# Turning rows with the DMA's transpose instead of TensorE in a feed-forward phase

## The chip, the cores and the metric

The kernel runs on one core of a Trainium2 chip. The core has five engines with queues of their own, which run side by side and wait for each other through semaphores: TensorE (PE in the profile), VectorE (DVE), ScalarE (ACT), GpSimd (POOL) and SyncE (SP), which here only starts DMAs. The metric is the time of one execution in microseconds of device time, as the median of several runs.

## The reference

64 sequences of 64 tokens, each token a row of 256 numbers (4096 rows in all), pass four layers. Each sequence b has a condition vector of 64 numbers.

1. A gated feed-forward layer with a quantized down projection, added to its input.
2. Attention with 16 heads inside each sequence, added to its input; and then the feed-forward that this document is about: with r = x / rms(x), gamma and beta vectors of the sequence,
   `x = x + alpha_b * ((silu(n Wg) * (n Wh)) Wo + bo)`, where `n = gamma_b * r + beta_b`. Wg and Wh are 256 x 1024, Wo is 1024 x 256.
3. A layer norm over the 256 numbers of a row, times a weight, plus a bias and a tanh vector of the sequence, times the weight again, plus the bias.
4. An adapter whose weights depend on the sequence: `x + relu(x Wd_b + bd) Wu_b + bu`, with Wd_b of 256 x 128 and Wu_b of 128 x 256.

Everything is float32. The large products are made of three matmuls each: both factors are split into a high part, rounded to the type fp32r, and the rest, and high x high, high x low and low x high are summed.

## The kernel before

The rows are worked in 8 blocks of 512. The first layer fills the first 255 us, attention the time to about 430 us, and the feed-forward with layer norm and adapter the rest. The change lies in that last phase.

There the main loop runs over n = 8 i + f: block i (0 to 7), and f (0 to 7), an eighth of the 1024 inner columns. The first five n are written out ahead of the loop. In iteration n:

- `f_inner` calls `f_products`: 12 matmuls of 512 columns on PE make the gate and the hidden half (`pg`, `pv`). ACT takes the silu of `pg` into `sg` (L816), DVE multiplies it by `pv` (L819).
- `f_parts` splits `sg`: ACT casts the high part (`hhi`, L856), DVE subtracts it (`hlo`, L857).
- `f_outer(n - 2)`: 12 matmuls of 256 columns add the columns of two iterations ago into `acc`.

Between these, spread over the iterations f, stands the work of other blocks:

- For block i+1, the rows are loaded (`f_load`, f=0), squared and summed by ACT with a root by POOL (`f_begin`, f=1), scaled by ACT into `xn` (`f_scale`, f=3), and turned in `norm_turn` for the two halves c of the 256 columns (f=5 and f=6): four PE transposes of 128 x 128 into a PSUM bank (L262), DVE's multiply by gamma into `xg` (L265), POOL's addition of beta (L266). At the head of the next iteration the function in `late` runs: ACT casts `xh` (L245) and POOL subtracts for `xl` (L246). The next block's products need both.
- For block i-1, DVE scales `acc` by alpha into `x3` (f=1), adds the input and takes the row statistics (f=1, f=2); POOL makes the root; DVE makes the shift `nm` (L896) and ACT centres four tiles (L898) in `f_center` (f=2); `f_adapt` (f=4, f=5) turns `x3` by four PE transposes per half (L933) between products and silu, and DVE scales the result into `x4` (L934).
- In f=7 PE runs one half of the up products of block i-2 (L979), then the down products of block i-1 from `x4` (`f_down`, L963), then the other up half. ACT takes the relu `dn`; DVE finishes `yo` (L995) and SP stores it.
- POOL adds common parts to the loaded adapter weights (`f_common`, L924: `wd` at f=7 and f=0, `wu` at f=3 and f=4) and to the block's input (`f_base`, f=7).

The order on PE, DVE, ACT and POOL is the order of the source (`manual_schedule`), also in the attention and feed-forward phases. SP is not among these engines after the opening part: there a scheduler puts its DMAs into an order of its own. Each queue runs in order, so an instruction that waits holds all behind it. Block 0 has no block before it, and in block 7 (`more` is false) nothing is prepared; its end is `f_last`.

The first layer already uses the DMA's transpose, for the 128 x 1024 quantized rows in bf16 (`quant`, L483), issued by SP. That transpose works on 16-bit elements.

Of the kernel before, what the change touches and what calls it, by code (L numbers as in the profile page):

```python
# [8 lines left out]
F32 = mybir.dt.float32  # L9
F32R = mybir.dt.float32r  # L10
BF16 = mybir.dt.bfloat16
AF = mybir.ActivationFunctionType
ALU = mybir.AluOpType
AX = mybir.AxisListType
# [3 lines left out]
P = 128  # L18
NB = 64
L = 64  # L20
D = 256
NTOK = NB * L
T = 512
NBLK = NTOK // T
BB = T // L
TT = T // P
# [10 lines left out]
def tile_kernel(ctx: ExitStack, tc, xT, x, condT, cw, upT, downT, qkvT, woT, ghT, outT_w,  # L37
                vecs, rows, g1, g2, gb, out):
    nc = tc.nc
# [12 lines left out]
    pools = {}  # L52
# [38 lines left out]
    def b3(ap):  # L91
        return ap.rearrange("p (b l) -> p b l", l=L)
# [165 lines left out]
    def norm_turn(xn, hl, i, c, vg, vb):  # L258

        pt = bank("mm")  # L260
        for t in range(TT):
            nc.tensor.transpose(pt[:, t * P:(t + 1) * P], xn[:, t, c * P:(c + 1) * P], ident)  # L262
        uid[0] += 1
        xg = main.tile([P, T], F32, tag="xg", bufs=2, name=f"xg{uid[0]}")
        nc.vector.tensor_tensor(b3(xg), b3(pt), bc(vg, c, i), ALU.mult)  # L265
        nc.gpsimd.tensor_tensor(b3(xg), b3(xg), bc(vb, c, i), ALU.add)  # L266
        return lambda: split(hl, c, xg, nc.gpsimd)

# [507 lines left out]
    def f_load(i):  # L776
        x2 = block(f"fx2_{i}")
        nc.sync.dma_start(out=x2, in_=tok(x2d, i))
        fblk[i] = dict(x2=x2)

    def f_begin(i):
        fblk[i]["rs"] = rms(fblk[i]["x2"], f"f{i}")

    def f_scale(i):
        fblk[i]["n"] = norm_tm(fblk[i]["x2"], fblk[i]["rs"], f"f{i}", True)
# [26 lines left out]
    def f_inner(n, between=lambda: None):  # L812
        pg, pv = f_products(n)
        between()
        sg = main.tile([P, T], F32, tag="st", bufs=2, name=f"sg{n}")
        nc.scalar.activation(sg, pg, AF.Silu)  # L816
        if n == LAST:
            return sg, pv
        nc.vector.tensor_tensor(sg, pv, sg, ALU.mult)  # L819
        return sg  # L820
# [71 lines left out]
    def f_center(i, tiles, rs):  # L892
# [3 lines left out]
        nc.vector.scalar_tensor_tensor(nm[:, :n], B["mv"][:, t0:t0 + n, 0], -1.0, rs[:, :n], ALU.mult, ALU.mult)  # L896
        for k, t in enumerate(tiles):
            nc.scalar.activation(B["x3"][:, t], B["x3"][:, t], AF.Identity, bias=nm[:, k:k + 1], scale=rs[:, k:k + 1])  # L898

# [27 lines left out]
    def f_adapt(i, c):  # L927
        B = fblk[i]
        if c == 0:
            B["x4"] = pools["c"].tile([P, 2, T], F32, tag="x4", bufs=2, name=f"x4_{i}")  # L930
        pt = bank("mm")
        for t in range(TT):
            nc.tensor.transpose(pt[:, t * P:(t + 1) * P], B["x3"][:, t, c * P:(c + 1) * P], ident)  # L933
        nc.vector.scalar_tensor_tensor(b3(B["x4"][:, c]), b3(pt), w2[:, c:c + 1], bc(V_LIN, c, i),  # L934
                                       ALU.mult, ALU.add)

    def f_turn(i, k):

# [241 lines left out]
    gbt = pools["c"].tile([P, 4, D], F32, tag="yo", bufs=1, name="gbt")  # L1180
    nc.sync.dma_start(out=gbt, in_=gb)
    late = []
    for n in range(5, N):
        i, f = divmod(n, 8)
        more = i + 1 < NBLK
# [4 lines left out]
        if i > 0 and f == 2:  # L1190
            f_added(i - 1, 1)
            f_stats(i - 1, 1)
            rln = rsqrt(fblk[i - 1]["mv"][:, :, 1], 1.0, 1e-5, f"ln{i - 1}")
        if i > 0 and f in (4, 5):
            sg = f_inner(n, lambda: f_adapt(i - 1, f - 4))
        else:
            sg = f_inner(n)
        if more and f in (5, 6):
            late = [norm_turn(*fblk[i + 1]["n"], i + 1, f - 5, V_FG, V_FB)]
        up = i - 2 if more and f == 7 else i - 2 if not more and f == 0 else -1  # L1200
        if up >= 0:
# [15 lines left out]
        if i > 0:  # L1217
            if f == 1:
                for k in range(2):
                    f_scaled(i - 1, k)  # L1220
                f_added(i - 1, 0)
                f_stats(i - 1, 0)
            if f == 2:
                f_center(i - 1, range(TT), rln)
        if i > 0 and more:
            if f == 0:
                f_load(i + 1)
            if f == 1:
                f_begin(i + 1)
            if f == 3:  # L1230
                f_scale(i + 1)
        if f == 2 and i > 0:
            f_rows(i)

        if f == (6 if more else 1):
            f_weights(i, "wd")
        if f == (7 if more else 1):
            f_weights(i, "wu")
# [70 lines left out]
```

## Time and profile before

| what | us |
|---|---|
| median of 3 runs | 743.86 (742.52 to 744.04) |
| the profiled execution | 743.25 |
| its span, first to last instruction | 741.5 |
| PE busy | 731.8 |
| DVE, ACT, POOL busy | 534.7, 412.6, 339.6 |
| DVE, ACT, POOL busy from 566 to 605, about one block | 22.54, 16.56, 20.87 |

A line of the timeline begins with the start and the duration in us, then the engine, the line of the source, the operation, what is written and read, the shapes, the number of merged instructions, and in brackets how long the engine stood idle before it and what released it. In a line of a group, the number before the comma behind the bar is the time in sum and the one behind it the mean in ns. Matmuls are pipelined: their durations overlap, and the distance of their starts says how fast they go.

### The profile page before, as it was taken

The numbers are of one execution on the slowest core, as the hardware profiler recorded it, in microseconds if no ns is written. First come the engines' busy times: TensorE is split into PE (matmuls) and PEld (weight loads), VectorE is DVE, ScalarE is ACT, GpSimd is POOL, SyncE is SP. The second block draws the span as 40 slices with busy tenths as digits, with TensorE's granted clock in tenths as the row PEclk, the third lists the DMA queues.
The fourth block names the chain that finished last, engine by engine and source line by source line (L and its number), as shares of the span: only waits on it lengthen the run. The fifth ranks groups of instructions, "written<-read, shape, count | busy, mean of one in ns | idle before, by whom it ended". The sixth has DMA issues, their size and how long they took to land.

```text
span 741.5 us, 17485 instructions
## 1 busy us (share of the span) xinstructions
PE 731.8 (99%) x7036; PEld 613.3 (83%) x7036; DVE 534.7 (72%) x827; ACT 412.6 (56%) x865; POOL 339.6 (46%) x359
## 2 busy tenths in 40 slices
PE   9999999999999999999999999999999999999997
PEld 8876766776686878998988888888889888888886
DVE  4998878867587688888888866656565555656566
ACT  6553446446455588998899674535353434434242
POOL 2123133143235436655555437464646464545292
PEclk9999999999999999999999999999999999999999
DMA  8898899999995974455665237713171809080821
GB/s 265 245 263 170 275 258 253 305 276 250 216 281 119 193 187 114 127 138 140 158 152 130 74 105 187 157 47 97 46 184 31 197 6 223 1 199 3 224 61 59
DMA packets 117457, 118.88 MB, mean 160 GB/s; under 512 B 39632, under 2 KB 101200, under 8 KB 117376
## 3 DMA queue, kind: packets, MB, share of 16 engines
q1 hardware_dynamic: 109232, 91.29, 50.4%
q0 software_dynamic: 7488, 25.37, 11.4%
q8 instruction: 55, 0.90, 0.5%
q10 hardware_dynamic: 656, 1.11, 0.5%
q14 instruction: 26, 0.21, 0.1%
HBM read 71.41 MB, written 29.56 MB: 136 GB/s over the span
## 4 chain that ended last, share of the span: by engine, by line
PE 83%; DVE 9%; ACT 3%; issue 2%; DMA 1%; POOL 0%; ACTq 0%; DVEq 0%; POOLq 0%
PE gh L89 7%; PE gh L88 7%; PE gh L87 7%; PE mm L87 6%; PE mm L89 6%; PE mm L88 6%; PE acc L87 4%; PE acc L88 4%; PE acc L89 4%; PE m L87 3%; PE m L89 3%; PE m L88 3%; PE mm L495 3%; PE m L712 3%; PE mm L304 3%; PE S L671 2%
## 5 line engine op out<-in xcount | busy, mean ns | idle before, releaser
L87 PE MATMUL mm<-up,xhl 128*128 128x512 f32 x240 | 97.2, 405 | 0.0
L87 PE MATMUL gh<-xhf,gh 128*128 128x512 f32 x244 | 95.3, 390 | 0.0
L89 PE MATMUL gh<-xhf,gh 128*128 128x512 f32 x244 | 95.1, 390 | 0.0
L88 PE MATMUL gh<-xlf,gh 128*128 128x512 f32 x244 | 95.1, 390 | 0.0
L89 PE MATMUL mm<-up,xll 128*128 128x512 f32 x240 | 93.9, 391 | 0.0
L88 PE MATMUL mm<-up,xhl 128*128 128x512 f32 x240 | 93.6, 390 | 0.0
L819 DVE TENSOR_TENSOR sg<-gh,sg 128x512 f32<-128x512 f32 x60 | 41.3, 688 | 62.1 <-PE gh L89 34.8
L469 ACT ACTIVATE g<-mm,rs_l 128x512 f32<-128x512 f32 x64 | 43.9, 690 | 69.8 <-PE mm L89 47.0
L857 DVE TENSOR_TENSOR hlo<-sg,hhi 128x512 fp32r<-128x512 f32 x58 | 56.2, 969 | 35.0 <-ACT hhi L856 33.7
L856 ACT CAST hhi<-sg 128x512 fp32r<-128x512 f32 x58 | 35.9, 620 | 76.4 <-DVE sg L819 75.2
L87 PE MATMUL acc<-wout,hhi 128*128 128x256 f32 x248 | 72.1, 291 | 0.0
L470 DVE SCALAR_TENSOR_TENSOR h<-mm,rs_l,g 128x512 f32<-128x512 f32 x64 | 46.4, 745 | 33.4 <-PE mm L89 24.0
L89 PE MATMUL acc<-wout,hlo 128*128 128x256 f32 x248 | 69.4, 280 | 0.6 <-DVE hlo L854 0.6
L88 PE MATMUL acc<-wout,hhi 128*128 128x256 f32 x248 | 69.4, 280 | 0.0
L266 POOL TENSOR_TENSOR xg<-xg,cv 128x512 f32<-128x512 f32 x32 | 33.1, 1042 | 65.8 <-DVE xg L265 65.8
L87 PEld LDWEIGHTS mm<-up,xhl 128*128 128x128 f32 x240 | 45.1, 188 | 15.2 <-issue 2.4
L89 PEld LDWEIGHTS gh<-xhf,gh 128*128 128x128 f32 x244 | 45.8, 188 | 9.7
L89 PEld LDWEIGHTS mm<-up,xll 128*128 128x128 f32 x240 | 45.0, 188 | 10.1
L88 PEld LDWEIGHTS mm<-up,xhl 128*128 128x128 f32 x240 | 45.2, 188 | 8.5
L88 PEld LDWEIGHTS gh<-xlf,gh 128*128 128x128 f32 x244 | 45.8, 188 | 7.3
L87 PEld LDWEIGHTS gh<-xhf,gh 128*128 128x128 f32 x244 | 45.8, 188 | 7.3
L816 ACT ACTIVATE sg<-gh 128x512 f32<-128x512 f32 x61 | 35.9, 589 | 26.1 <-PE gh L89 26.1
(259 smaller groups left out, 1930.3 us busy)
## 6 DMA issues: line engine op xcount, KB each, us to landing
gt<-in_g SPq DMA_DIRECT2D x32, 512.0 KB, 7.5
rows<-alphad SPq DMA_DIRECT2D x48, 256.0 KB, 5.5
vb<-vx SPq DMA_DIRECT2D x32, 256.0 KB, 5.3
wd<-s1d SPq DMA_DIRECT2D x32, 256.0 KB, 6.1
wu<-s2d SPq DMA_DIRECT2D x32, 256.0 KB, 6.0
xt<-in_x SPq DMA_DIRECT2D x8, 512.0 KB, 7.6
s1d<-stgs POOLq DMA_DIRECT2D x16, 256.0 KB, 7.0
s1d<-stg POOLq DMA_DIRECT2D x16, 256.0 KB, 6.9
```

The costliest lines, as they stand in the source:

```text
L87: nc.tensor.matmul(out, lhsT=l[0], rhs=r[0], start=first, stop=False)
L88: nc.tensor.matmul(out, lhsT=l[0], rhs=r[1], start=False, stop=False)
L89: nc.tensor.matmul(out, lhsT=l[1], rhs=r[0], start=False, stop=last)
L266: nc.gpsimd.tensor_tensor(b3(xg), b3(xg), bc(vb, c, i), ALU.add)
L304: nc.tensor.matmul(pb[s][c * 64:(c + 1) * 64], lhsT=gl[h], rhs=gt[h, c * GC:(c + 1) * GC], start=True, stop=True, tile_position=(64 * s, 6 ...
L469: nc.scalar.activation(g, pg, AF.Gelu, scale=rs[:, t:t + 1])
L470: nc.vector.scalar_tensor_tensor(h[:, ch * 512:(ch + 1) * 512], pv, rs[:, t:t + 1], g, ALU.mult, ALU.mult)
L495: nc.tensor.matmul(py[:, :D], lhsT=qt[:, f, :], rhs=wq[:, f, :], start=f == 0, stop=f == 7)
L816: nc.scalar.activation(sg, pg, AF.Silu)
L819: nc.vector.tensor_tensor(sg, pv, sg, ALU.mult)
L856: nc.scalar.copy(h_hi, sg)
L857: nc.vector.tensor_tensor(h_lo, sg, h_hi.bitcast(F32), ALU.subtract)
```

## The change

In the feed-forward loop the PE transposes of the next block's rows (blocks 2 to 7) and of the adapter's input (blocks 0 to 6) are replaced by three steps.

- `split_words`: ACT copies a float32 tile of 128 x 1024 as 16-bit words, all low halves and then all high halves, into `planes`: two instructions of 1024 elements.
- `turn_words`: SP issues two DMA transposes from SBUF to SBUF, one for each set of halves, into `turned`.
- `join_words`: for each half c of the columns, DVE copies 1024 16-bit words so that low and high halves stand side by side again, as 512 float32 numbers.

`norm_joined` takes the place of `norm_turn`: join, DVE's multiply in place, POOL's addition, and the same function for `late`. `f_adapt` joins into `x4` and then scales in place. Where the steps stand in a block i between 1 and 6:

| step | before | after |
|---|---|---|
| load of rows | block i+1 at f=0 | block i+2 at f=4 |
| squares and root | block i+1 at f=1 | block i+2 at f=7 |
| scale into `xn` | f=3 | f=0 |
| split and transposes of rows | - | f=1 |
| turned rows to `xg`, both halves | f=5, f=6, between sg and the split of n | f=4, f=5, behind the split of n |
| shift `nm` | f=2 | f=2 |
| centring on ACT | f=2, at the end | f=3, between silu and the cast of n |
| split and transposes of `x3` | - | f=4 |
| `x4`, both halves | f=4, f=5, PE between products and silu | f=6, at the end |
| `wd` loads | f=6 | f=5 |

In block 0 the rows of block 1 are still turned by PE, and block 2 is loaded at f=5. In block 7 the steps of `x3` stand at the same f. `planes` and `turned` take buffers that attention used. From n = 5 on SP too follows the order of the source.

```diff
+    def split_words(src, name):
+        planes = pools["b"].tile([P, 16, L], F32, tag="ex2", bufs=2, name=f"planes_{name}")
+        dst = planes.rearrange("p a l -> p (a l)").bitcast(U16).rearrange("p (h c t f) -> p h c t f", h=2, c=2, t=TT)
+        words = src.rearrange("p t d -> p (t d)").bitcast(U16).rearrange("p (t c f h) -> p h c t f", t=TT, c=2, h=2)
+        for h in range(2):
+            nc.scalar.copy(dst[:, h], words[:, h])
+        return planes
+    def turn_words(planes, name):
+        turned = pools["b"].tile([P, 2, 512], F32, tag="pts", bufs=2, name=f"turned_{name}")
...
+        for h in range(2):
+            nc.sync.dma_start_transpose(out=dst[:, h], in_=src[:, h])
+        return turned
+    def join_words(dst, turned, c):
+        src = turned.rearrange("p c n -> p (c n)").bitcast(U16).rearrange("p (h c n) -> p h c n", h=2, c=2)
+        nc.vector.tensor_copy(dst.bitcast(U16).rearrange("p (n h) -> p h n", h=2), src[:, :, c])
+    def norm_joined(hl, turned, i, c, vg, vb):
+        xg = main.tile([P, T], F32, tag="xg", bufs=2, name=f"xg{uid[0]}")
+        join_words(xg, turned, c)
+        nc.vector.tensor_tensor(b3(xg), b3(xg), bc(vg, c, i), ALU.mult)
         nc.gpsimd.tensor_tensor(b3(xg), b3(xg), bc(vb, c, i), ALU.add)
         return lambda: split(hl, c, xg, nc.gpsimd)
...
-        pt = bank("mm")
-        for t in range(TT):
-            nc.tensor.transpose(pt[:, t * P:(t + 1) * P], B["x3"][:, t, c * P:(c + 1) * P], ident)
-        nc.vector.scalar_tensor_tensor(b3(B["x4"][:, c]), b3(pt), w2[:, c:c + 1], bc(V_LIN, c, i),
-                                       ALU.mult, ALU.add)
+        x4 = B["x4"][:, c]
+        join_words(x4, B["turned"], c)
+        nc.vector.scalar_tensor_tensor(b3(x4), b3(x4), w2[:, c:c + 1], bc(V_LIN, c, i), ALU.mult, ALU.add)
...
+    ordered.close()
+    ordered.enter_context(tc.manual_schedule(engines=engines | {E.SP}))
     for n in range(5, N):
...
-        if i > 0 and f in (4, 5):
-            sg = f_inner(n, lambda: f_adapt(i - 1, f - 4))
-        else:
-            sg = f_inner(n)
-        if more and f in (5, 6):
-            late = [norm_turn(*fblk[i + 1]["n"], i + 1, f - 5, V_FG, V_FB)]
+        sg = f_inner(n)
+        if i == 0 and f in (5, 6):
+            late = [norm_turn(*fblk[1]["n"], 1, f - 5, V_FG, V_FB)]
+        if i > 0 and f == 3:
+            f_center(i - 1, range(TT), rln, shift)
...
             if f == 2:
-                f_center(i - 1, range(TT), rln)
+                shift = f_shift(i - 1, range(TT), rln)
+            if f == 4:
+                fblk[i - 1]["turned"] = turn_words(split_words(fblk[i - 1]["x3"], f"x{i - 1}"), f"x{i - 1}")
+            if f == 6:
+                for c in range(2):
+                    f_adapt(i - 1, c)
         if i > 0 and more:
             if f == 0:
-                f_load(i + 1)
+                f_scale(i + 1)
             if f == 1:
-                f_begin(i + 1)
-            if f == 3:
-                f_scale(i + 1)
+                fblk[i + 1]["turned"] = turn_words(split_words(fblk[i + 1]["n"][0], f"n{i + 1}"), f"n{i + 1}")
+            if f in (4, 5):
+                late = [norm_joined(fblk[i + 1]["n"][1], fblk[i + 1]["turned"], i + 1, f - 4, V_FG, V_FB)]
+        if i + 2 < NBLK:
+            if f == (4 if i else 5):
+                f_load(i + 2)
+            if f == 7:
+                f_begin(i + 2)
...
-        if f == (6 if more else 1):
+        if f == (5 if more else 1):
             f_weights(i, "wd")
```

More of the change, by code (lines that the diff above doesn't have):

```diff
@@ L11 @@
 BF16 = mybir.dt.bfloat16
+U16 = mybir.dt.uint16
 AF = mybir.ActivationFunctionType
@@ L265, in norm_turn @@
         nc.vector.tensor_tensor(b3(xg), b3(pt), bc(vg, c, i), ALU.mult)
+        nc.gpsimd.tensor_tensor(b3(xg), b3(xg), bc(vb, c, i), ALU.add)
+        return lambda: split(hl, c, xg, nc.gpsimd)
+    def split_words(src, name):
[7 more added lines that the diff above has]
+        turned = pools["b"].tile([P, 2, 512], F32, tag="pts", bufs=2, name=f"turned_{name}")
+        src = planes.rearrange("p a l -> p (a l)").bitcast(U16).rearrange("p (h n) -> p h n", h=2)
+        dst = turned.rearrange("p c n -> p (c n)").bitcast(U16).rearrange("p (h k r) -> p h k r", h=2, k=8)
+        for h in range(2):
[5 more added lines that the diff above has]
+    def norm_joined(hl, turned, i, c, vg, vb):
+        uid[0] += 1
+        xg = main.tile([P, T], F32, tag="xg", bufs=2, name=f"xg{uid[0]}")
+        join_words(xg, turned, c)
+        nc.vector.tensor_tensor(b3(xg), b3(xg), bc(vg, c, i), ALU.mult)
         nc.gpsimd.tensor_tensor(b3(xg), b3(xg), bc(vb, c, i), ALU.add)
@@ L810, in f_products, with f_inner @@
         return pg, pv
-    def f_inner(n, between=lambda: None):
+    def f_inner(n):
         pg, pv = f_products(n)
-        between()
         sg = main.tile([P, T], F32, tag="st", bufs=2, name=f"sg{n}")
@@ L890, in f_stats, with f_shift @@
             nc.vector.bn_aggr(B["mv"][:, t], B["st"][:, t])
-    def f_center(i, tiles, rs):
+    def f_shift(i, tiles, rs):
         B, n, t0 = fblk[i], len(tiles), tiles[0]
@@ L896, in f_center @@
         nc.vector.scalar_tensor_tensor(nm[:, :n], B["mv"][:, t0:t0 + n, 0], -1.0, rs[:, :n], ALU.mult, ALU.mult)
+        return nm
+    def f_center(i, tiles, rs, nm=None):
+        B = fblk[i]
+        nm = f_shift(i, tiles, rs) if nm is None else nm
         for k, t in enumerate(tiles):
```

## The prediction

> **What bounds the kernel now.** I read the page first: its busy times and the chain that ended last.
>
> ```profile
> span 741.5 us, 17485 instructions
> PE 731.8 (99%) x7036; PEld 613.3 (83%) x7036; DVE 534.7 (72%) x827; ACT 412.6 (56%) x865; POOL 339.6 (46%) x359
> ...
> PE 83%; DVE 9%; ACT 3%; issue 2%; DMA 1%; POOL 0%; ACTq 0%; DVEq 0%; POOLq 0%
> ```
>
> PE is busy throughout and carries 83% of the chain. The same chain in order of time gives the rhythm of the feed-forward phase: the adapter's down products (L963) come once a block.
>
> ```profile
> 604.65 1.08 PE mm L979 x32
> 605.74 1.87 PE mm L963 x64
> 607.60 0.93 PE mm L979 x32
> 643.53 1.08 PE mm L979 x32
> ```
>
> A block lasts 643.53 - 604.65 = 38.9 us, and in this phase the chain stays on PE to the last block. Then the timeline, PE first, to price a transpose:
>
> ```profile
> 521.97 0.39 PE L89 MATMUL gh<-xhf,gh 128*128 128x512 f32 x1
> ...
> 522.20 0.60 PE L262 MATMUL mm<-ident,xnf 128*128 128x128 f32 x4
> ...
> 522.55 0.37 PE L87 MATMUL acc<-wout,hhi 128*128 128x256 f32 x1
> ...
> 522.75 0.28 PE L88 MATMUL acc<-wout,hhi 128*128 128x256 f32 x1
> ```
>
> Durations of matmuls overlap, so the start times count: four transposes put the next product 0.35 us later, and 0.08 us more are lost at the change of kind. By the starts of the gate products, an iteration without a turn takes 4.13 us, with one 4.56, with two 5.03.
>
> Last the other engines, where a turned row passes DVE, POOL and ACT:
>
> ```profile
> 596.97 0.68 DVE L819 TENSOR_TENSOR sg<-gh,sg 128x512 f32<-128x512 f32 x1
> 597.57 0.68 DVE L265 TENSOR_TENSOR xg<-mm,cv 128x512 f32<-128x512 f32 x1
> 598.34 1.58 DVE L857 TENSOR_TENSOR hlo<-sg,hhi 128x512 fp32r<-128x512 f32 x1
> ...
> 598.32 1.04 POOL L266 TENSOR_TENSOR xg<-xg,cv 128x512 f32<-128x512 f32 x1 [6.37 <-DVE xg L265]
> ...
> 599.39 0.62 ACT L245 CAST xhf<-xg 128x512 fp32r<-128x512 f32 x1 [1.09 <-POOL xg L266]
> 599.92 0.59 ACT L816 ACTIVATE sg<-gh 128x512 f32<-128x512 f32 x1
> ```
>
> Two things are to be seen. ACT's silu (L816) waits in its queue behind the cast of the turned rows (L245), and so for POOL's add and DVE's multiply. And a DVE instruction with two SBUF inputs (L857) that starts beside a POOL one takes 1.58 us, where it takes 0.69 alone: it ran after POOL's.
>
> **What is removed.** 48 transposes of block rows (L262 has 56 in this phase, the 8 for block 1 stay) and 56 of the adapter (L933): 26 groups of four. Blocks 1 to 6 have four groups each, by the iterations above 2 x (4.56 - 4.13) + (5.03 - 4.13) = 1.75 us; block 7 has two, 0.9. Sum 6 x 1.75 + 0.9 = **-11.4 us**, all on the path, since PE has no other idle time there.
>
> **What is added.** The groups of 1024 elements, shapes kept apart:
>
> ```profile
> L684 DVE TENSOR_TENSOR ex<-S,mx 128x1024 f32<-128x1024 f32 x32 | 39.2, 1224 | 1.1
> L481 DVE TENSOR_SCALAR q<-h 128x1024 bf16<-128x1024 f32 x32 | 24.1, 754 | 1.1
> ...
> L689 ACT ACTIVATE ex<-ex 128x1024 f32<-128x1024 f32 x32 | 34.1, 1066 | 12.4 <-DVE ex L684 12.4
> ```
>
> ACT: 26 splits of 1024 elements, by L689 1.07 us each; 4.3 us a block beside 16.6 busy of 39. DVE: 26 joins of 1024 16-bit elements, from SBUF to SBUF with one input. Rows from both sides: L481, one input, in SBUF, 0.69 as its median; L684, from PSUM, 1.22. The join has one input and both ends in SBUF, as L481, so I take 0.69 and keep 1.22. The multiplies that follow had PSUM and SBUF inputs and now have two in SBUF; their durations stay (0.68, 0.74), but they can meet POOL. SP: 26 transposes of the shape of the existing one:
>
> ```profile
> L483 SPq DMA_TRANSPOSE qt<-q x32: 1231/1358/5807, 23.0 to 250.2; - x32
> ...
> DMA to landing us min/median/max: 3.0/5.9/17.8
> ```
>
> That is 1.36 us of SP each and 5.9 to landing, in a phase where the DMA engines are 94% busy; in the feed-forward phase they are 45% busy.
>
> **What moves.** On SP the source order now holds. In block i: two transposes of rows (f=1), four row loads (f=2), two of the adapter (f=4), then the block load, four wd loads, and at f=7 two stores and four wu loads. The load of block i+2 and the wd loads stand behind the adapter's transposes, which wait for ACT. By the walk below these are issued by 25.5 us, five issues of about 0.6 follow, and wd lands (6.1) near 35; POOL wants it past 40, behind the root that follows the squares of f=7. Cost nothing; without that cover POOL's bias adds slip, and they have a block's length to spare. The 30 us that SP spent on row loads waiting for POOL (L277) go, and nobody on the path waited for them. The squares (f=1 to f=7), the scale (f=3 to f=0) and the centring (behind the silu of f=3) keep their ACT time; PE doesn't wait for them directly.
>
> **Where it hurts: the order on DVE and ACT.** Before, PE turned the rows while DVE was between sg and hlo, and the adapter input was ready at f=5. Now the join stands behind hlo in f=4 and f=5, and both adapter joins behind hlo(6), right before PE's down products of f=7 want them. I walk one block from its first gate product (571.09 in the trace), without transposes: iteration f starts at 4.13 f, f=7 at 28.9, and down is due after products and one up half: 28.9 + 2.83 + 0.98 = 32.7.
> The centring's shift ends at 17.1 and centring at 19.2, as now (L896, L898). ACT then casts hhi(3), 19.8, and DVE subtracts, 20.5, so sg(4) starts at 20.4. From sg to the next free DVE slot behind hlo is 1.98 (594.32 to 596.30). Join 0.62 with its handover, multiply to POOL 0.75 (597.57 to 598.32), POOL to cast 1.07, cast to silu 0.53, silu to sg 0.63: one loop is 5.6 us against 4.13 of PE. So sg(5) at 26.0 and sg(6) at 31.6; hlo(5) falls on POOL's wu adds or its subtraction and pays the 0.89 seen above: 32.45. Then hlo(6) ends and the joins begin at 34.45; join, x4, join, x4 (0.62, 0.66, 0.62, 0.75) end at 37.1. PE waits 37.1 - 32.7 = **4.4 us in each of blocks 2 to 6**, and 5.4 in block 1, which has no up half before it: 27.4 us. Behind the waiting down products stand the other up half and the outer products of f=5; behind the joins on DVE sg(7) and both yo, so a late transpose would hold these too. Bounds of one wait: 3.5 if hlo(5) meets no POOL instruction; 6.5 with joins of 1.22; 9 if two more instructions wait for a POOL add of 1.26 each.
>
> **The tail.** In block 7 the adapter's four DVE instructions stand before the last sg. DVE now waits 0.62 us there, so 2.7 - 0.6 = 2.1 us come on top; POOL adds without pause then, and each of the four may wait up to 1.26: up to 7. I take **+4**.
>
> **PE's clock.** It is 1.00 in all rows. The longest PE gap now is 1.65 us (before 228.07), and the products after it start 0.23 us apart, the full rate. At the start of the span, after idling, matmuls of the transposes' shape (L507) start 0.24 apart, where transposes take 0.09, and the full rate comes at about 9 us. So a gap of 4.4 costs between 0 and half of those 8 us, 4; I take 1 each, near the 1.65 us gap, **+6**.
> [...]
>
> **Sum.** -11.4 + 27.4 + 4 + 6 = +26.0 on the profiled execution of 743.25 (span 741.5 and 1.75 around it): 769.3. The median of the runs is 0.6 above that execution: **770 us**, 3.5% slower.
>
> **Rivals.** (a) No wait: DVE's 22.5 busy us of a block grow only to 25.3 of 37.1, and if the queues ran ahead of PE the gain would stand: 743.9 - 11.4 + 2.1 = 735. Against it: the loop of 5.6 us is a chain, not a load. It decides below (11.4 - 4) / 6 = 1.2 us of wait per block. Chance 0.08. (b) Joins at one element a cycle, 1.22: waits 6 x 6.5 + 1 = 40, so 743.9 - 11.4 + 40 + 5 + 6 = 783. For: strided 16-bit output, which no row has. 0.2. (c) The clock falls fully at each wait, 4 instead of 1: 770 + 18 = 788. 0.12. (d) The adapter's transposes land late: the second is issued at about 24.5 and joined at 34.45, so from 10 us on it decides; at the worst row, 17.8, each block waits 8 more: 770 + 48 = 818. Against: idle DMA engines. 0.07. (e) Gain and wait cancel: 744. 0.02. The forecast holds the other 0.51.
>
> **Range.** 0.2%, 1.5 us, is about what runs from 742.52 to 744.04 can tell from no change. Low end: waits of 3.5 (22), tail 2.1, no clock loss: 743.9 + 12.7 = 757, a little below it for shorter lag; high end: (b) and most of (c) together, 798. 754 to 798 leaves out (a), (d) and (e). Slower is (b), (c), (d) and the forecast: 0.9; faster is (a).
>
> **What would show it.** After: no L262 or L933 transposes past block 1; PE gaps before L963 in blocks 1 to 6, released by DVE's x4, of 4 to 6 us, and a block of 37.1 + 4.4 = 41.5 us; joins at 0.69; silu late behind the cast in f=5 and f=6; a granted clock below 1.00 if (c). It would be wrong if x4 came before PE's up half ended, or if the wait's releaser were a DMA.

## The result and the profile after

The changed kernel takes 787.4 us (median of 4 runs, 786.8 to 788.5) where the kernel before takes 743.5 (742.5 to 744.0): a ratio of 1.059, with a 95% interval of 1.0575 to 1.0612. It is 5.9% slower. Ratios here and below leave out runs over 1.5% above their kernel's fastest, of which there is one. The prediction had the sign and the place, and was 17 us short.

The profiled execution has a span of 785.0 us, 43.5 more than the 741.5 before. The page of the kernel after, first the busy times, then the granted clock in 40 slices, then the chain that ended last:

```profile
span 785.0 us, 17412 instructions
...
PE 737.5 (94%) x6932; PEld 618.7 (79%) x6932; DVE 555.2 (71%) x853; ACT 435.0 (55%) x891; POOL 346.8 (44%) x359
...
PEclk9999999999999999999999999898989899897998
...
PE 59%; DVE 19%; issue 9%; ACT 6%; POOL 5%; DMA 2%; DVEq 0%; ACTq 0%; POOLq 0%
```

PE's share of the chain falls from 83% to 59%; DVE's rises from 9% to 19%, ACT's from 3% to 6% and POOL's from 0% to 5%. PE's busy time is no smaller although 104 transposes are gone: the clock row, which was full speed throughout, has a dent about once per block from the 26th slice on (0.50 from 535.34 to 542.16 us in block 2), and matmuls take longer in it.

One block of the timeline of the kernel after, PE around f=7 (start, duration, what, and in brackets the idle time and its releaser). L1015 are the up products, L999 the down products:

```profile
531.44 1.15 PE L1015 MATMUL mm<-dn,wu 128*64 128x64 f32 x32
536.35 0.48 PE L999 MATMUL mm<-x,wd 128*64 128x64 f32 x4 [3.76 <-issue]
537.75 3.47 PE L999 MATMUL mm<-x,wd 128*64 128x64 f32 x60 [0.91 <-DVE x L971]
541.00 1.63 PE L1015 MATMUL mm<-dn,wu 128*64 128x64 f32 x32
```

PE waits for the first half of x4, does four matmuls, waits for the second half, and then runs slowly. (The profile names no releaser for the first gap, "issue"; DVE's multiply that completes this half, L971, ends at 536.25.) The two gaps are 3.76 + 0.91 us; with the four matmuls between them the down products are held up for about 5 us. After them the second up half takes 1.56 us by the starts, where it took 1.03 before. The table of windows shows why (columns: the stretch, its length, busy time and instructions of PE, PEld, DVE, ACT and POOL, granted clock, DMA share, GB/s):

```profile
527.00:532.60 5.60, 5.59 (x58) 4.67 (x56) 3.10 (x3) 1.28 (x3) 2.85 (x4) 1.00 0.98 274
532.60:536.30 3.70, 0.00 (x0) 0.00 (x0) 2.84 (x5) 1.22 (x3) 0.96 (x1) 0.87 0.00 0
536.30:541.00 4.70, 3.74 (x65) 3.58 (x66) 2.62 (x4) 0.00 (x0) 0.00 (x0) 0.50 0.15 56
541.00:544.00 3.00, 3.00 (x48) 2.93 (x47) 0.84 (x2) 1.32 (x3) 0.00 (x0) 0.81 0.02 5
```

The clock drops to one half near the end of the wait and stays there through the down products: by the three windows' shortfalls, (0.13 x 3.7 + 0.5 x 4.7 + 0.19 x 3.0) / 0.5 = 6.8 us at half speed.

What PE waits for is best read in the chain of waits in order of time (start, length, what), here for the block that ends near 677 us:

```profile
656.88 1.05 POOL xg L299
...
657.95 0.02 ACT xhf L246
657.97 0.50 issue
658.48 0.60 ACT sg L848
...
659.10 0.70 DVE sg L851
...
659.83 0.63 ACT hhi L888
...
660.48 1.73 DVE hlo L889
662.21 0.67 DVE xg L291
...
662.90 0.70 DVE xg L298
...
663.68 1.05 POOL xg L299
...
667.88 0.74 DVE x L291
```

This is the loop of the prediction, in one piece: POOL's addition, ACT's cast (L246) and the silu behind it (L848), sg, hhi, hlo on DVE, the join (L291), the multiply (L298), and POOL again. This turn takes 663.68 - 656.88 = 6.8 us, where PE's iteration takes 4.13; it is the dearer of two, because hlo meets POOL's subtraction and takes 1.73, where it takes 0.69 alone. The turn before it, from sg(4) to sg(5), takes 5.8. The two together put the adapter's joins behind the time at which the down products are due.

The new instructions themselves, from the groups with their shapes kept apart (mean ns of one behind the busy time):

```profile
L291 DVE COPY x<-turned_x 128x1024 uint16<-128x1024 uint16 x14 | 14.6, 1042 | 0.0
...
L291 DVE COPY xg<-turned_n 128x1024 uint16<-128x1024 uint16 x12 | 9.0, 749 | 0.0
...
L276 ACT COPY planes_x<-x 128x1024 uint16<-128x1024 uint16 x13 | 13.0, 1042 | 0.0
```

The same join is on average dearer for the adapter than for the rows: four of the fourteen, in block 6 and the tail, take 1.8 us, the others 0.73 to 0.74. The tail shows the reason, DVE beside POOL's bias additions, and PE behind it:

```profile
757.83 1.85 DVE L291 COPY x<-turned_x 128x1024 uint16<-128x1024 uint16 x1
759.71 1.60 DVE L971 SCALAR_TENSOR_TENSOR x<-x,w,cv 128x512 f32<-128x512 f32 x1
761.24 1.80 DVE L291 COPY x<-turned_x 128x1024 uint16<-128x1024 uint16 x1
763.07 1.59 DVE L971 SCALAR_TENSOR_TENSOR x<-x,w,cv 128x512 f32<-128x512 f32 x1
...
765.49 0.58 PE L88 MATMUL acc<-wout,hhi 128*128 128x256 f32 x1 [5.31 <-ACT hhi L884]
```

Where the time went, by the starts of products. Each f=7 stretch is from the gate products of f=7 to those of the next f=0.

| stretch | before | after | difference |
|---|---|---|---|
| iterations with turns (26 groups of four transposes) | | | -11.4 |
| f=7 of block 1 | 6.34 | 14.55 | +8.2 |
| f=7 of blocks 2 to 5, each | 8.20 | 15.4 | 4 x 7.2 = +28.8 |
| f=7 of block 6 | 8.20 | 19.32 | +11.1 |
| tail: block 7's last outer products, to the start of the down products | 5.87 | 13.02 | +7.15 |
| sum | | | +43.9 |

The spans differ by 43.5.

### The profile page after: what moved, and what is told of

The parts are those of the page before. It is cut to its first block, busy times and chain, and to the rows that moved or that the text cites. A ratio compares the mean times of both kernels' runs of the same rounds, so it can differ in the third digit from the quotient of the medians.

```text
span 785.0 us, 17412 instructions
## 1 busy us (share of the span) xinstructions
PE 737.5 (94%) x6932; PEld 618.7 (79%) x6932; DVE 555.2 (71%) x853; ACT 435.0 (55%) x891; POOL 346.8 (44%) x359
## 4 chain that ended last, share of the span: by engine, by line
PE 59%; DVE 19%; issue 9%; ACT 6%; POOL 5%; DMA 2%; DVEq 0%; ACTq 0%; POOLq 0%
PE mm L88 6%; PE mm L90 6%; PE mm L89 6%; PE m L88 3%; PE m L90 3%; PE m L89 3%; PE m L745 3%; PE mm L528 3%; PE gh L90 3%; PE gh L89 3%; PE gh L88 3%; PE mm L337 3%; PE mm L999 3%; POOL wu L962 2%; PE acc L88 2%
## 5 line engine op out<-in xcount | busy, mean ns | idle before, releaser
L889 DVE TENSOR_TENSOR hlo<-sg,hhi 128x512 fp32r<-128x512 f32 x58 | 51.9, 895 | 53.2 <-ACT hhi L888 53.0
L999 PE MATMUL mm<-x,wd 128*64 128x64 f32 x448 | 25.5, 302 | 34.2 <-issue 20.6
L88 PEld LDWEIGHTS acc<-wout,hhi 128*128 128x128 f32 x248 | 47.3, 191 | 7.9 <-ACT hhi L884 5.5
L90 PEld LDWEIGHTS gh<-xhf,gh 128*128 128x128 f32 x244 | 45.8, 188 | 9.6
L962 POOL TENSOR_TENSOR wd<-wd,bias 128x512 f32<-128x512 f32 x32 | 52.1, 1649 | 0.0
L999 PEld LDWEIGHTS mm<-x,wd 128*64 128x64 f32 x448 | 23.4, 210 | 36.4 <-issue 21.4
```

Of the source, the lines that this page charges most:

```text
L88: nc.tensor.matmul(out, lhsT=l[0], rhs=r[0], start=first, stop=False)
L90: nc.tensor.matmul(out, lhsT=l[1], rhs=r[0], start=False, stop=last)
L889: nc.vector.tensor_tensor(h_lo, sg, h_hi.bitcast(F32), ALU.subtract)
L962: nc.gpsimd.tensor_tensor(w[:, 2 * h:2 * h + 2], w[:, 2 * h:2 * h + 2], row.unsqueeze(1).broadcast_to([P, 2, D]), ALU.add)
L999: nc.tensor.matmul(pd[s * 64:(s + 1) * 64, (b - b0) * L:(b - b0 + 1) * L], lhsT=B["wd"][b // 4][:, b % 4, c, s * 64:(s + 1) * 64], rhs=B[" ...
```

## The experiments

All ratios are to the kernel before, with 95% intervals. "After" is the changed kernel.

### The clock: work put into the wait

```diff
 def f_down(i, half=None):
     pd = bank("mm" if half is None else "acc")
+    for _ in range(22 if i + 2 < NBLK else 0):
+        nc.tensor.matmul(pd, lhsT=pools["gh"][0][:, 0, :P], rhs=fblk[i + 1]["n"][1][0][:, 0], start=True, stop=True)
```

> The changed kernel with 22 matmuls of 128x512 added ahead of the down products of blocks 0 to 5, into the bank that the down products then overwrite: they give PE about 5 us of work (22 at 0.23 us) in the time in which it would wait for x4, and leave the result alone. Theory (idle time halves the clock, and the half clock costs 2 to 2.5 us behind each wait): the granted clock stays at 1.00 in blocks 1 to 6, the 64 down products take 1.9 us again instead of 4.65 and the total falls by 8 to 14 us although work is added: 773 to 779. Rival (the products behind the wait are slow for another reason, such as cold weights loads or x4's arrival): 786 to 792, down products at 4.6 us as now.

Measured: 778.2 us (777.4 to 782.7), ratio 1.048 (1.045 to 1.051). With 132 matmuls added the kernel is 9 us faster than after. PE of this kernel, the fillers in the first line, and a window over a block and a half:

```profile
533.20 5.28 PE L997 MATMUL mm<-xhf,gh 128*128 128x512 f32 x22
538.41 0.34 PE L1001 MATMUL mm<-x,wd 128*64 128x64 f32 x4
539.29 1.97 PE L1001 MATMUL mm<-x,wd 128*64 128x64 f32 x60 [0.54 <-DVE x L971]
541.09 1.10 PE L1017 MATMUL mm<-dn,wu 128*64 128x64 f32 x32
```

```profile
540.00:600.00 60.00, 60.00 (x509) 52.96 (x506) 33.74 (x58) 29.40 (x60) 31.73 (x26) 1.00 0.53 124
```

The clock is 1.00 and 60 down products take 1.8 us by the starts (539.29 to 541.09) instead of 3.25 (537.75 to 541.00). In blocks 3 to 5 the f=7 stretch falls from 15.4 to 13.5. So of the 7.2 us that a block loses there, 1.9 are the clock's and 5.3 are the wait itself. The expectation was not met everywhere: in blocks 1 and 6, where gaps of 1.8 and 4.1 us in sum were left, the clock still fell for 3.4 us.

### One half of the change at a time

Rows only (the adapter on PE as before):

```diff
-        sg = f_inner(n)
+        sg = f_inner(n, lambda: f_adapt(i - 1, f - 4, True)) if i > 0 and f in (4, 5) else f_inner(n)
...
-            if f == 4:
-                fblk[i - 1]["turned"] = turn_words(split_words(fblk[i - 1]["x3"], f"x{i - 1}"), f"x{i - 1}")
-            if f == 6:
-                for c in range(2):
-                    f_adapt(i - 1, c)
```

> The block rows keep their DMA transposes, splits and joins; the adapter's input is turned by PE again in f=4 and f=5, between products and sg, as before the change (its splits and DMA transposes are left out). Theory: the adapter's joins at the end of f=6 are what PE waits for; without them the down products find x4 ready, the PE wait of 4.9 us and the lower clock of blocks 1 to 6 go, the tail is as before (5.9 us), and of the 11.4 us that the removed transposes were worth the rows' half, 5.3, is kept: 736 to 742. Rival (the join of the rows behind hlo slows the loop of sg by itself, so that PE waits for hhi or hlo in the outer products instead): 750 to 775, with the wait moved to the outer products of f=6 and f=7.

Adapter only (the rows on PE as before):

```diff
-        if i == 0 and f in (5, 6):
-            late = [norm_turn(*fblk[1]["n"], 1, f - 5, V_FG, V_FB)]
+        if more and f in (5, 6):
+            late = [norm_turn(*fblk[i + 1]["n"], i + 1, f - 5, V_FG, V_FB)]
...
-            if f == 1:
-                fblk[i + 1]["turned"] = turn_words(split_words(fblk[i + 1]["n"][0], f"n{i + 1}"), f"n{i + 1}")
-            if f in (4, 5):
-                late = [norm_joined(fblk[i + 1]["n"][1], fblk[i + 1]["turned"], i + 1, f - 4, V_FG, V_FB)]
```

> The adapter's input keeps its DMA transposes, splits and joins at the end of f=6; the block rows are turned by PE again in f=5 and f=6, with the multiply between sg and hlo, as before the change (their splits and DMA transposes are left out). Theory (both together make the wait: rows delay sg(6), adapter joins stand behind it): sg(6) is on time, joins begin near 33 us of the block and end near 36, and the down products are due near 33.5, so a wait of 1.5 to 3 us is left in a block, too short to lower the clock; the tail keeps its 7 us: 748 to 768. Rival 1 (the adapter's joins alone make the whole wait): waits of 5 us, clock lowered, 780 to 790. Rival 2 (only the rows make it): no wait, 742 to 748 with the tail.

Measured: rows only 749.3 us, ratio 1.008 (1.007 to 1.010); adapter only 763.5, ratio 1.027 (1.025 to 1.029). Alone they cost 6.0 and 20.1, together 44: 18 us come from their meeting, as the theory of the second run says. The waits of that run are down to 0.42 and 0.90 us in blocks 3 to 5, with the clock at 1.00 there; blocks 1, 2 and 6 and the tail keep longer ones. That a wait of 1.5 to 3 us is too short to lower the clock was my estimate, and block 2 does not bear it out: behind 1.30 + 0.90 us the clock was 0.50 from 533.3 to 536.7.

The rows' expectation was missed: x4 was in time, yet PE found a wait that neither theory had named. The timeline of that kernel:

```profile
529.09 0.68 DVE L852 TENSOR_TENSOR sg<-gh,sg 128x512 f32<-128x512 f32 x1
529.69 0.74 DVE L1038 SCALAR_TENSOR_TENSOR yo<-mm,vc,x 128x512 f32<-128x512 f32 x1
...
530.48 1.15 PE L1022 MATMUL mm<-dn,wu 128*64 128x64 f32 x32 [1.34 <-DVE yo L1038]
```

The second up half needs the PSUM bank that DVE empties with the first yo (L1038), and this stands behind sg(6), hlo(6) and sg(7), all late by the loop. Waits of 1.3 to 2.0 us a block eat the 0.87 that the rows' transposes were worth.

### What makes the loop: join ahead of hlo, or cast behind hhi

Join early:

```diff
         sg = f_inner(n)
+        if i > 0 and more and f in (4, 5):
+            late = [norm_joined(fblk[i + 1]["n"][1], fblk[i + 1]["turned"], i + 1, f - 4, V_FG, V_FB)]
...
-            if f in (4, 5):
-                late = [norm_joined(fblk[i + 1]["n"][1], fblk[i + 1]["turned"], i + 1, f - 4, V_FG, V_FB)]
```

> One thing is moved: the join of block i+1's rows is emitted right behind sg of f=4 and f=5, ahead of hhi and hlo, instead of at the end of the iteration. The transposes by DMA, splits and joins all stay, and the adapter's joins stay at the end of f=6. Theory (order of the queue, not the work, makes the wait): the loop from sg to sg loses hlo's place in it and falls from 5.8 us to under PE's 4.13, so sg(6) comes near 31.2 us after the block's first product instead of 33.05, the last x4 near 36 and PE's wait before the down products falls from 5.3 to between 1.6 and 3.5 us; block period 44.4 -> 39 to 41.5 us; total 787 -> 752 to 770. Rival 1 (DVE simply has too much work in these iterations): x4 comes as late as before, and the total stays at 780 to 790. Rival 2 (the wait is on the adapter's DMA transposes): x4's joins wait for a DMA, nothing changes, 785 to 790.

Measured: 774.6, 774.7, 784.5 and 787.3 us, ratio 1.047 (1.040 to 1.054). sg(6) came 31.5 us after the block's start and the waits of blocks 2 to 5 were as foreseen, 2.23 + 1.06 us, but the loop was not broken and the total missed its range. POOL and ACT of this kernel:

```profile
526.80 1.43 POOL L299 TENSOR_TENSOR xg<-xg,cv 128x512 f32<-128x512 f32 x1 [0.62 <-DVE xg L298]
...
528.26 0.62 ACT L246 CAST xhf<-xg 128x512 fp32r<-128x512 f32 x1 [3.78 <-POOL xg L299]
528.78 0.59 ACT L848 ACTIVATE sg<-gh 128x512 f32<-128x512 f32 x1
```

The silu still stands behind the cast, and the cast waits 3.78 us for POOL: from sg(5) at 523.13 to sg(6) at 529.41 the loop takes 6.3 us, without hlo in it. And the clock fell at these waits too, except in block 3. PE in blocks 2 and 3, and four windows of 3.41 us, two in each block:

```profile
533.02 0.34 PE L999 MATMUL mm<-x,wd 128*64 128x64 f32 x4 [2.23 <-issue]
534.41 3.17 PE L999 MATMUL mm<-x,wd 128*64 128x64 f32 x60 [1.06 <-DVE x L971]
...
575.07 0.34 PE L999 MATMUL mm<-x,wd 128*64 128x64 f32 x4 [2.23 <-issue]
576.46 1.97 PE L999 MATMUL mm<-x,wd 128*64 128x64 f32 x60 [1.06 <-DVE x L971]
```

```profile
530.28:533.69 3.41, 0.85 (x22) 0.60 (x18) 2.83 (x5) 0.97 (x2) 0.00 (x0) 1.00 0.00 0
533.69:537.10 3.41, 2.69 (x50) 2.69 (x52) 1.93 (x3) 0.00 (x0) 0.00 (x0) 0.50 0.19 68
571.24:574.65 3.41, 1.60 (x35) 1.11 (x33) 2.47 (x4) 1.30 (x3) 1.05 (x1) 1.00 0.35 86
574.65:578.06 3.41, 1.93 (x58) 1.83 (x60) 2.99 (x5) 0.00 (x0) 0.00 (x0) 1.00 0.00 0
```

The same two gaps cost 3.17 us of down products in one block and 1.97 in the next. The windows show why. In the trace of after the clock changes only at the borders of a fixed row of steps of 3.41 us (it falls at 490.96, 535.34 and 579.71 us, 13 steps apart), and these windows, as long as a step, are each at 1.00 or 0.50 throughout. In block 2 the gaps leave PE idle for 3.41 - 0.85 = 2.56 us of one step, and the next step runs at 0.50. In block 3 they fall on both sides of a border, 1.81 us in one step and 1.48 in the other, and the clock stays. The first three runs of this kernel spread over 10 us, where those of the changed kernel spread over 1.7, and the longest of the three had the lowest mean clock (0.969, the other two 0.978); that the place of the borders makes this spread was not separated.

Cast late:

```diff
-        for rest in late:
-            rest()
-        late = []
+        rests, late = late, []
...
         f_parts(n, sg)
+        for rest in rests:
+            rest()
```

> One thing is moved in the changed kernel: ScalarE's cast of the joined rows (and POOL's subtraction after it) is emitted behind hhi of the next iteration instead of ahead of its silu; the joins stay at the ends of f=4, f=5 and f=6. Theory (the loop runs over the cast: join, multiply, POOL's add, cast, silu, sg, and this is what makes sg(5) and sg(6) late): the silus follow PE again, sg(6) comes near 28.5 us of the block instead of 33.05, the adapter's joins near 30.5, x4 near 33.5 where the down products are due at 32.7: a wait of 0 to 1.5 us, no lower clock in blocks 1 to 5, block period 44.4 -> 38 to 40; the tail keeps its 7 us. 744 to 758. Rival 1 (DVE's amount of work): sg(6) stays later than 31 us, 765 to 785. Rival 2 (the adapter's DMA transposes, which land near 29 us of the block, are next): the joins wait for a DMA, x4 near 36, 765 to 775.

Measured: 780.0 us (777.4 to 780.8), ratio 1.048 (1.046 to 1.050). The silu of f=6 now follows PE, and sg(6) comes 30.2 us after the block's start instead of 33.05. But x4 ends at 36.2, only 1.8 earlier than the 38.0 of after. DVE and POOL of this kernel:

```profile
525.84 1.24 DVE L889 TENSOR_TENSOR hlo<-sg,hhi 128x512 fp32r<-128x512 f32 x1 [0.69 <-ACT hhi L888]
527.00 1.85 DVE L291 COPY xg<-turned_n 128x1024 uint16<-128x1024 uint16 x1
528.89 1.62 DVE L298 TENSOR_TENSOR xg<-xg,cv 128x512 f32<-128x512 f32 x1
530.43 0.68 DVE L851 TENSOR_TENSOR sg<-gh,sg 128x512 f32<-128x512 f32 x1
...
532.40 1.82 DVE L291 COPY x<-turned_x 128x1024 uint16<-128x1024 uint16 x1
...
525.24 2.99 POOL L962 TENSOR_TENSOR wu<-wu,bias 128x512 f32<-128x512 f32 x2
528.18 1.77 POOL L247 TENSOR_TENSOR xlf<-xg,xhf 128x512 fp32r<-128x512 f32 x1
```

Four instructions beside POOL's take 1.24, 1.85, 1.62 and 1.82 where the same ones take 0.69, 0.75, 0.69 and 0.74 alone: 3.7 us of collisions replace the loop. Neither theory is whole. The rival's 31 us for sg(6) was not reached, but its cause, DVE, is what holds x4; only it is not DVE's amount of work but its meeting POOL. In blocks 2 to 5 waits of 2.0 to 2.9 + about 1 us remain, and the clock falls in them (in block 3 it is 0.50 from 577.0 to 583.9 us), so that little of the total is won.

### The tail

In addition to the late cast, the last block's adapter input on PE:

```diff
+        ... f_inner(n, lambda: f_adapt(i - 1, f - 4, True)) if not more and f in (4, 5) else f_inner(n)
-            if f == 4:
+            if f == 4 and more:
                 fblk[i - 1]["turned"] = turn_words(split_words(fblk[i - 1]["x3"], f"x{i - 1}"), f"x{i - 1}")
-            if f == 6:
+            if f == 6 and more:
```

> The kernel with the late cast, and in the last block (block 7, whose adapter pass is for block 6) the adapter's input is turned by PE in f=4 and f=5 as before the change, without its split, its DMA transposes and its joins. Theory (the tail's 7.15 us are the four DVE instructions next to POOL's bias adds, 1.85 + 1.60 + 1.80 + 1.59 = 6.84): the tail from the last group of outer products of f=6 to the last block's products is 5.9 us again, 6 to 8 us less than the kernel with the late cast alone; 737 to 750. Rival (the tail waits for the wu and wd additions of POOL themselves or for the new place of the load): 2 us less or nothing.

Measured: 772.8 us (771.4 to 776.7), ratio 1.038 (1.037 to 1.040). The total missed its range with the late cast's; the difference, 780.0 - 772.8 = 7.2 us, is what the theory gave to the tail, and the tail's PE gap of 5.3 us is gone, with the clock at 1.00 in the tail. So the four DVE instructions were its cause. Their 6.84 us are not the 7.15 themselves, though: PE's wait in after is 5.31 us where before had 0.57, 4.7 more, and the other 2.4 us are lost at the half clock that follows (0.50 from 764.0 to 770.9 us).

### SP in source order alone

```diff
 (in the kernel before)
     late = []
+    ordered.close()
+    ordered.enter_context(tc.manual_schedule(engines=engines | {E.SP}))
     for n in range(5, N):
```

> The kernel before, with nothing turned by DMA and nothing moved, but SP held to the source order from n=5 on as in the changed kernel. Theory (the order of SP's queue costs nothing, as predicted): 742.0 to 745.0, no new PE gap. Rival (row loads or weight loads are held up behind waiting stores): POOL's bias adds or the row sums slip, and the time is 747 or more.

Measured: 743.6 us, ratio 1.000 (0.9988 to 1.0012). The order alone costs nothing; the run has no DMA transposes in that queue.

### Repairs: give PE other work while DVE is late

Down in f=0 of the next block, the rest as in after:

```diff
                 f_up_store(up, pus, chunks=range(1))
-                if more:
+                if i == NBLK - 2:
                     f_down(i - 1)
...
-        elif more and i > 0 and f == 7:
-            f_down(i - 1)
...
             f_outer(n - 2, range(2 if n - 2 in KEPT else TT))
+        if f == 0 and 1 < i < NBLK - 1:
+            f_down(i - 2)
```

> The changed kernel with one thing moved on PE: the down products of blocks 0 to 4 are emitted in f=0 of the next block, behind its outer products, instead of in f=7; nobody reads their result before f=7 of that next block. DVE, ScalarE, POOL and the DMAs keep the changed kernel's order. Down is then due near 28.9 + 2.83 + 2.0 + 1.4 + 2.8 + 1.4 = 39.3 us of the block and x4 ends near 38. Theory (the price of the change is an order that puts x4 behind its due time, no lack of any engine): the waits of blocks 1 to 5 and their lower clock go; the block period falls from 44.4 to 37.5 to 39.5; block 6 and the tail stay as they are: 787 less about 5 x 6 = 755, 746 to 762. Rival (DVE is late by more than x4, so that the outer products wait for hhi and hlo of f=6 and f=7 instead): PE gaps of 3 us or more before outer products in f=0 and f=1, 770 to 785.

Measured: 768.9 us, ratio 1.034 (1.032 to 1.036). Between theory and rival. The block period falls from 44.4 to 40.6 and the clock is 1.00 in blocks 2 to 5, but two smaller waits take the place of the large one. PE of this kernel, with the lines of one block:

```profile
537.19 2.09 PE L999 MATMUL mm<-x,wd 128*64 128x64 f32 x64 [1.78 <-DVE yo L1031]
...
547.34 0.36 PE L88 MATMUL acc<-wout,hhi 128*128 128x256 f32 x1 [0.98 <-DVE x L911]
```

Down now waits for the bank that yo frees, and the first outer products of the new block for DVE's reading of the old sums (L911). Both stand on DVE behind the delayed joins. Block 6, whose down was left in place, waits 8.2 + 2.8 us.

The order mended throughout: down in f=0, the cast behind hhi from block 1 on, and blocks 6 and 7 with the adapter on PE (edits as above, with `i >= NBLK - 2` for the last two blocks):

> The changed kernel with its order mended: down of blocks 0 to 4 in f=0 of the next block, the cast of the joined rows behind hhi from block 1 on, and in blocks 6 and 7, where no later place is free, the adapter's input turned by PE in f=4 and f=5 as before the change. Theory: no PE wait over 1.5 us is left, clock 1.00, the tail 5.9 us; of the 11.4 us that the removed transposes were worth, 1.75 (blocks 6 and 7) are given back: 743.3 - 11.4 + 1.8 = 733.7; 732 to 739, faster than the kernel before. Rival (DVE, with 2.8 us of joins and 1.3 us more of collisions with POOL in a block, is late elsewhere): 744 to 760.

Measured: 746.4 us, ratio 1.0043 (1.0028 to 1.0058): 41 us less than after, but 7 above the theory's range and inside the rival's. A wait before the first outer products of each new block, for DVE's reading of the old sums, was left: 1.61 us once, then 0.97 in each block. So down was moved one iteration further, to where this wait is:

```diff
-        if f == 0 and 1 < i < NBLK - 1:
+        if f == 1 and 1 < i < NBLK - 1:
             f_down(i - 2)
```

> The kernel with the mended order, down one iteration later still: in f=1 of the next block, behind the outer products of f=7, instead of in f=0. In the run with f=0 PE waited 0.97 us in each block before the first outer products of the new block, for DVE's reading of the two outer banks, which stood behind the joins' delay and had no down products as cover. Theory: the 1.9 us of down products cover this wait; the block period falls from 38.84 to 37.7 to 38.0 and the total by 4 to 6 us to 740 to 742.5, no better than rows by DMA with the adapter by PE (739.75). Rival 1 (the wait for the banks only moves, or the iterations stretch by DVE's amount of work): 745 to 747. Rival 2 (with no wait left the whole 0.87 us of each pair of turned halves is won): 735 to 738.

Measured: 738.1 us (736.9 to 739.6), ratio 0.9934 (0.9921 to 0.9948). It is 0.7% faster than the kernel before. The time lies between the theory, which had 740 to 742.5, and the second rival, 735 to 738. One block of it in the table of windows:

```profile
528.10:565.60 37.50, 37.50 (x322) 33.06 (x321) 28.56 (x41) 19.84 (x39) 23.14 (x19) 1.00 0.59 141
```

PE is busy for all of the 37.5 us at full clock, where a block took 38.9 before. DVE is busy 28.6 us in it, more than the 24.5 of a block after and the 22.5 before, and PE waits for nothing.

The smaller repair keeps the adapter on PE and only moves the cast of the rows:

> Rows by DMA, adapter's input by PE, as in the run with the rows only, and the cast of the rows emitted behind hhi of the next iteration. That run had x4 in time, and PE waited 1.4 us in each block for the first yo, which on DVE stood behind a late sg(6) and sg(7). Theory: with the silus on time the 1.4 us go, the block period falls from 39.7 to 38.0 to 38.4 (38.87 before the change) and the total to 736 to 741. Rival (a join and a multiply more on DVE are too much whatever the order): the wait before the second up half stays over 1 us, 747 to 750.

Measured: 741.3 us, ratio 0.9968 (0.9956 to 0.998), against 749.3 with the cast in its old place. The wait for yo was gone, the block period 38.1; but block 1 lost 1.4 us at its second gate products, which waited for the last subtraction of its own rows. With the old place kept in block 0:

```diff
         rests, late = late, []
+        if i == 0:
+            for rest in rests:
+                rest()
+            rests = []
```

> The rows by DMA, the adapter by PE, the cast late as in the run of that name, but for block 0, where the cast stays ahead of the next products: in that run PE waited 0.86 us in block 1 for the late subtraction and the iteration took 5.51 us for 4.13. Theory: 1.4 us less, 739.3 to 740.5. Rival (the subtraction is late for another reason): 741 as in that run.

Measured: 739.8 us, ratio 0.9952 (0.9937 to 0.9967), as expected. The two repaired kernels are 1.6 us apart and their intervals overlap, so which of them is faster stays open.

## Why the prediction was right, and where it was short

**The removal: right.** Iterations f=4 to f=6 of blocks 1 to 6 take 4.13 us in the changed kernel; the 11.4 us are there, and they are spent again.

**The prices of the new operations: right where they run alone.** A join takes 0.75 us (0.69 taken), a split 1.04 (1.07). The pair of transposes takes SP 2.6 us (2.7 taken), and they land in 3.2 us instead of 5.9; no wait in blocks 1 to 6 names them. Rival (b), joins at 1.22, and rival (d), late transposes, are out. What failed here is the upper bound of the join: beside POOL it takes 1.8, and the 1.22 row from PSUM said nothing on that (1.22 is what L684 took; that it stands for one element a cycle no run shows).

**SP's order: right**, by the run that has it alone, and in the changed kernel by the waits: none of PE's in blocks 1 to 6 ends on a DMA.

**The walk through the queues: right in its places, a little short.** For block 2, from its first products at 499.69 us:

| event | foreseen | measured |
|---|---|---|
| shift of the centring ends | 17.1 | 17.2 |
| sg(4) | 20.4 | 20.5 |
| sg(5) | 26.0 | 26.2 |
| sg(6) | 32.45 | 33.05 |
| adapter's joins begin | 34.45 | 35.0 |
| x4 complete | 37.1 | 38.0 |
| down products held up | 4.4 | 5.3 |

The loop was named as join, multiply, POOL, cast, silu, sg; moving the cast alone let the silus follow PE, and moving hlo alone did not. Of the 0.9 us that were missing, 0.6 are four joins that take 0.77 from start to start for 0.62, and 0.16 are hlo(5), 1.74 for 1.58.

**Block 6: wrong, a term that was not there.** I gave it the wait of the others, 5.4 us with the clock, and it lost 11.1. In block 6 the adapter's four DVE instructions meet POOL's wd and row additions and take 6.8 us (1.79, 1.60, 1.80, 1.59) instead of 3.0. The upper bound of 9 us for a wait was met there: PE idled 6.2 + 2.8 us. The prediction had POOL's wd additions "behind the root that follows the squares of f=7", and in blocks 2 to 5 they are: POOL stands idle while the joins run (from 533.56 to 546.00 in block 2). Block 6 has no rows of a block 8 to square, so no root holds POOL back and its additions start at 711.01, just ahead of the joins. I had seen that an instruction beside POOL takes 0.9 us more, had used it once, for hlo(5), and had not asked at each new place on DVE what POOL does then.

**The tail: wait right, clock left out.** The range was 2.1 to 7, I took 4; it was 7.15. Of these, 4.7 are PE's longer wait, close to the 4, and 2.4 are the half clock behind it, which the sum priced for six waits and not for this one. "Each of the four may wait" was the right reading: all four did, since POOL adds there without pause, which the trace of before shows from 705.24 to 725.25.

**The clock: under-priced.** I took 1 us a wait from a 1.65 us gap that had cost nothing, over the 4 from the start of the span. The filler run puts it at 1.9 in each of blocks 3 to 5. What a longer gap costs the trace of the kernel before does not show; the runs do. In the changed kernel the clock is at 0.50 in seven stretches ahead of the last one, which the end of the trace cuts off: six of 6.83 us and one of 10.24, two and three times 3.41. PE need not idle for all of the 3.41 us ahead of such a stretch: 2.69 were enough in the changed kernel and 2.56 in the run with the early join, so waits under 3.4 us were punished too. And in that run the same gap of 2.23 + 1.06 us was punished in block 2, where 2.56 us of it fell into one step, and not in block 3, where it fell into two with 1.81 and 1.48. Rival (c) came out at 788 and the measurement at 787, but not by its reason: the clock costs half of what it assumed, and block 6 and the tail make up the rest.

**The sum.** Predicted +26.0: -11.4, 27.4 of waits, 4, 6. Measured by stretches +43.9. The missing 17.9: 4 x (7.2 - 5.4) = 7.2 in blocks 2 to 5, 8.2 - 6.4 = 1.8 in block 1, 5.7 in block 6, 3.15 in the tail. That 787 lies in the range is in part luck: the part of the range above the forecast stood there for dear joins in every block (b) and a fully priced clock (c), and neither came.

**What would have shown it wrong** did not come: no DMA released PE, and x4 never came before the up half ended. Of the signs named for it, DVE's x4 behind the waits and the silu behind the cast came; the PE gaps were 4.7 us in blocks 2 to 5, as named, but 6.6 in block 1 and 9.0 in block 6, and the block was 44.4 us instead of 41.5. The clock below 1.00, named as the sign of rival (c), came without (c)'s price.

## What to carry to other kernels

An engine that is idle for two fifths of a block, as DVE was before the change (22.5 us busy of 38.9), can still be late in every block: work moved onto it must be placed, not only afforded, and the question for each new instruction is what stands behind it in its queue and who waits for that. Here nearly the same move of work (the adapter's turns of two of its seven blocks went back to PE) was 5.9% slower in one order and 0.7% faster in another, in which PE's down products, whose result nobody needs for a block, stand where DVE is late, and ScalarE's cast no longer holds the silu. When a wait is removed, walk on to the next thing that the late engine owes, down to the PSUM banks that it must empty.

## What the runs showed of the hardware

- A copy of 1024 16-bit elements with a stride on its output takes 0.75 us on VectorE alone and 1.79 to 1.86 beside a GpSimd addition (1.32 beside the end of one, in the run with the early join at 523.74); the multiplies behind it 0.69 and 0.75 alone, 1.6 beside. I had expected this only of instructions with two inputs in SBUF, from L857's 1.58 for 0.69 in the kernel before. In the run with the late cast the join that starts at 527.00 ends at 528.85, 0.6 us after the GpSimd additions that end at 528.23; what holds it up until then no run shows.
- In the changed kernel the granted clock changes only in steps of 3.41 us (it falls at 490.96, 535.34, 579.71, 624.08 and 668.46 us, each time 13 steps later), and the clock of a step went with the time that PE idled in the step before, by the profile's busy times. There each of the eight steps at full clock with 2.69 us or more of idle time was followed by one at 0.50, and every one with 1.26 or less by 1.00. In the kernel before the most in a step at full clock that was followed by another is 1.59; in the run with the early join 2.56 were followed by 0.50 and 1.81 by 1.00. At half speed less idle time was enough to stay there: in the changed kernel each of the eight steps with 1.46 us or more was followed by another at 0.50, and each of the seven with 0.68 or less by 1.00. Two short waits counted together where they fell into one step (1.30 + 0.90 us in block 2 of the adapter alone: 0.50 from 533.3 to 536.7), and waits of 1.4 us (rows only, blocks 2 to 5) went free.
- Matmuls without use, 22 in each of six waits, made the changed kernel 9 us faster (778.2 for 787.4).
